# Moving the second stage's constants, first convolutions and first time step into the attention stage, with shared pools and single probability buffers

## The chip, the cores and the metric

The kernel runs on one core of one Trainium2 chip. The core has a matmul engine (TensorE, PE in the profile, with its weight loads shown as PEld), three engines for element-wise work (VectorE = DVE, ScalarE = ACT, GpSimd = POOL), and SyncE (SP), which issues nearly all transfers. Each engine works through its own instructions in program order; semaphores make one wait for another. All arithmetic is in 32-bit floats. The metric is the device time of one execution in microseconds: 3513.71 us, the median of three runs (3506.32 to 3513.76).

## What is computed

The input x has 8 sequences of 512 positions and 512 channels. Each position is layer-normed to xn, and two branches read xn: a selective state-space layer s, and a feed-forward layer whose gate is modulated by causal attention (16 heads of 32). Cut to what matters:

```python
xn = layernorm(x)
# attention, only as a rank-16 modulation of the gate
q, k, v = heads(rms(xn, ln1) @ Wq.T), heads(... Wk.T), heads(... Wv.T)
probs = softmax(causal(q @ k.T / sqrt(32)))
mod = 0.1 * tanh((probs @ v) @ Wo.T @ A)
h = rms(xn, ln2)
gate = silu(h @ W_in_base.T + mod * (h @ A) @ B)
g = silu(xn + (gate * (h @ W_up_base.T)) @ W_down.T)
# state space: 1024 channels, 16 states each
u, z = split(xn @ W_in.T)
xc = silu(causal_conv4(u) + conv_b)
B, C, dt = split(xc @ W_x.T);  dt = softplus(dt + mean(dt_bias))
h_t = exp(-exp(A_log) * dt_t) * h_{t-1} + dt_t * B_t * xc_t     # over 512 positions
s = ((sum_n C_t h_t + D * xc) * silu(z)) @ out_W.T
out = x + s * g
```

## The kernel before: how it is tiled and staged

There are two stages in one program, and both write their instructions in an order laid out by hand (a manual schedule): each engine runs what the Python code emits, in that order.

**Stage one** (the block with the pools a_w, a_row, a_big, a_small, a_p, a_ps_s, a_ps_mm, lines 80 to 489) does the norms and the attention for all eight sequences. Its unit is a group: one sequence b and one set hg of four heads, 32 groups in all. In group g the loop over s = 0..3 emits, for the group's own heads, `scores` for the s-th block of 128 queries (matmuls L292, mask L298, maximum L302, exponentials L308), and beside them, for the group before, ten `turn_probs` (four transposes each, L325, copied out at L331 on ACT or L329 on DVE), and, for the group before that, `divide` (L351 to L358). The list `slots` puts further products in between: queries and keys of the next group (L274), values (L258), transposes of the next sequence (L239). At the end of the group comes `attend` (L338) for the group before. `beside` places the norms of the next sequence and its loads. Exponentials are emitted two and three pieces after their scores. `modulation` (L366 to L376) closes each sequence and stores its 16 rows to the scratch scr_m; the transposed norms go to the scratch scr_x.

Products go to a ring of two PSUM banks (`bank`, pool a_ps_mm); scores go to three tiles of two banks each (a_ps_s). The probabilities of the s-th query block lie in a tile with tag p0 to p3 that has two buffers; the transposed ones in pt0 to pt3 with one each.

**Between the stages**, once stage one's pools are closed (from line 492 on): SP loads the constants of stage two (`const_tile`, L507), a_log is transposed (L536), stored (L540) and read back spread out by 16 loads (an, L543), the matrix sel is made by POOL and summed by DVE (L573 to L578), and the mean of dt_bias is formed (L564 to L568). Then the queue of parts for sequence 0 runs with nothing beside it: eight `conv_in` (product L590, bias L646, three taps L629, tanh L633, product with the sum L637, store to scr_c L641), and `step_size`: four projections (L792), softplus (L805 to L822), and a turn that stores to scr_p (L831) and loads bb, cc and dt (L833 to L837). The load of sequence 0's h and modulation (`load_h`, L518 and L521) is issued after the convolutions. Then come the first four scan inputs (L869).

**Stage two** (the loop at the end of the kernel) walks 64 scan steps per sequence: a scan on DVE (L898) over two channels' groups of states, decays on ACT (L878), products with B on DVE (L890) or POOL (L892) in turn, with C on POOL (L905), and sums over states on PE (L917). Between them it works off a queue of parts: gate products (`z_gate`, first one first, L590 and L658), `gate_up` (L678 to L704), the previous sequence's `finish` (L729, L745), and the next sequence's convolutions and step size. Its PSUM pool ps_mm is a ring of four banks; y, decay and a copy of B hold the other four.

Of the kernel before, what the change touches and what calls it, by code (L numbers as in the profile page):

```python
# [17 lines left out]
P = 128  # L18
NB = 8
# [20 lines left out]
def mamba_gated_ffn_kernel(  # L40
# [39 lines left out]
    with ExitStack() as c1:  # L80
        wp = c1.enter_context(tc.tile_pool(name="a_w", bufs=1))
        row = c1.enter_context(tc.tile_pool(name="a_row", bufs=8))
        big = c1.enter_context(tc.tile_pool(name="a_big", bufs=2))
        sm = c1.enter_context(tc.tile_pool(name="a_small", bufs=6))
        pp = c1.enter_context(tc.tile_pool(name="a_p", bufs=2))
        ps_s = c1.enter_context(tc.tile_pool(name="a_ps_s", bufs=3, space=PSUM))
        ps_mm = c1.enter_context(tc.tile_pool(name="a_ps_mm", bufs=2, space=PSUM))

        c1.enter_context(tc.manual_schedule())

        ZW = NH * R + R
        xts = {}

        def load_x(b):
            xts[b] = []
            for tt in range(TT):
                xt = row.tile([P, DM], F32, tag="xt", name=f"xt_{b}_{tt}")
                nc.sync.dma_start(xt, x[b, ts(tt, P), :])
                xts[b].append(xt)

        load_x(0)
        ln1 = wp.tile([P, KT], F32, tag="ln1", name="ln1")
        nc.sync.dma_start(ln1, ln1_w)
        ln2 = wp.tile([P, KT], F32, tag="ln2", name="ln2")
        nc.sync.dma_start(ln2, ln2_w)
        a_sb = wp.tile([P, KT, R], F32, tag="a_sb", name="a_sb")
        nc.sync.dma_start(a_sb, lora_a)
        wo = pp.tile([P, KT, DM], F32, tag="p3", name="wo")
        nc.sync.dma_start(wo, w_o)
        wv = pp.tile([P, KT, DM], F32, tag="p3", name="wv")  # L110
        nc.sync.dma_start(wv, w_v)
        wq = wp.tile([P, HG, KT, P], F32, tag="wq", name="wq")
        nc.sync.dma_start(wq, w_q)
        wk = wp.tile([P, HG, KT, P], F32, tag="wk", name="wk")
        nc.sync.dma_start(wk, w_k)

        eps_ln = wp.tile([P, 1], F32, tag="eps_ln", name="eps_ln")
        nc.vector.memset(eps_ln, LN_EPS)
        eps_rms = wp.tile([P, 1], F32, tag="eps_rms", name="eps_rms")
        nc.vector.memset(eps_rms, RMS_EPS)  # L120

        mask = wp.tile([P, P], F32, tag="mask", name="mask")
        nc.gpsimd.memset(mask, 0.0)
        nc.gpsimd.affine_select(
            out=mask, in_=mask, pattern=[[-1, P]], compare_op=ALU.is_ge,
            fill=MASKED, base=0, channel_multiplier=1,
        )


        zs = []  # L130
        for i in range(2):
            z = wp.tile([P, TT, HG, 4, 2 * R], F32, tag=f"z{i}", name=f"z{i}")
            nc.gpsimd.memset(z, 1.0)
            zs.append(z)
        woab = wp.tile([P, HG, 4, R], F32, tag="woab", name="woab")
        nc.gpsimd.memset(woab, 0.0)
        wz = wp.tile([P, KT, ZW], F32, tag="wz", name="wz")

        scale = 1.0 / math.sqrt(HD)

        xnT, xhT, norm, qks, probs, pts, outs, has, mos = {}, {}, {}, {}, {}, {}, {}, {}, {}

        def bank(name):
            return ps_mm.tile([P, 512], F32, tag="mm", name=name)

        def fold_weights():

            for hg in range(HG):
                ps = bank(f"ps_woa_{hg}")
                for jt in range(KT):  # L150
                    nc.tensor.matmul(
                        ps[:, :R], lhsT=wo[:, jt, ts(hg, P)], rhs=a_sb[:, jt, :],
                        start=(jt == 0), stop=(jt == KT - 1),
                    )
                for h in range(4):
                    nc.vector.tensor_copy(woab[ts(h, HD), hg, h, :], ps[ts(h, HD), :R])
            wvt = big.tile([P, HG, DM], F32, tag="hT", name="wvt", bufs=1)
            for hg in range(HG):
                ps = bank(f"ps_wvt_{hg}")
                for kt in range(KT):  # L160
                    nc.tensor.transpose(ps[:, ts(kt, P)], wv[:, kt, ts(hg, P)], ident)
                nc.scalar.copy(wvt[:, hg, :], ps)
            for kt in range(KT):
                ps = bank(f"ps_wz_{kt}")
                for hg in range(HG):
                    nc.tensor.matmul(
                        ps[:, ts(hg, 4 * R)], lhsT=wvt[:, hg, ts(kt, P)],
                        rhs=woab[:, hg].rearrange("p h r -> p (h r)"), start=True, stop=True,
                    )
                nc.vector.tensor_scalar(  # L170
                    wz[:, kt, : NH * R], ps[:, : NH * R], ln1[:, kt : kt + 1], None, ALU.mult
                )
                nc.vector.tensor_scalar(
                    wz[:, kt, NH * R :], a_sb[:, kt, :], ln2[:, kt : kt + 1], None, ALU.mult
                )
            for w, f in ((wq, scale), (wk, 1.0)):
                for kt in range(KT):
                    nc.vector.tensor_scalar(
                        w[:, :, kt, :], w[:, :, kt, :], ln1[:, kt : kt + 1], f,
                        ALU.mult, ALU.mult,  # L180
                    )

        def statistics(b):

            st = {}

            def moments(tt):
                if tt == 0:
                    st["mv"] = sm.tile([P, TT, 2], F32, tag="mv", name=f"mv_{b}")
                bn = sm.tile([P, nc.vector.BN_STATS_DIM], F32, tag="bn", name=f"bn_{b}_{tt}")  # L190
                nc.vector.bn_stats(out=bn, in_=xts[b][tt])
                nc.vector.bn_aggr(out=st["mv"][:, tt, :], in_=bn)

            def deviation():
                st["sd"] = sm.tile([P, TT], F32, tag="sd", name=f"sd_{b}")
                nc.scalar.activation(st["sd"], st["mv"][:, :, 1], AF.Sqrt, bias=eps_ln)

            def variance():
                mv = st["mv"]
                rstd = stats[:, b, :, 1]  # L200
                nc.vector.reciprocal(rstd, st["sd"])
                v2 = sm.tile([P, TT], F32, tag="v2", name=f"v2_{b}")
                nc.vector.tensor_tensor(v2, mv[:, :, 1], rstd, ALU.mult)
                nc.vector.tensor_tensor(v2, v2, rstd, ALU.mult)
                st["v2"] = v2

            def root():
                st["sd2"] = sm.tile([P, TT], F32, tag="sd2", name=f"sd2_{b}")
                nc.scalar.activation(st["sd2"], st["v2"], AF.Sqrt, bias=eps_rms)

            def ends():
                nc.vector.tensor_copy(stats[:, b, :, 0], st["mv"][:, :, 0])
                rs2 = sm.tile([P, TT], F32, tag="rs2", name=f"rs2_{b}")
                nc.vector.reciprocal(rs2, st["sd2"])
                norm[b] = [rs2]

            return [lambda tt=tt: moments(tt) for tt in range(TT)], [
                deviation, variance, root, ends,
            ]

        def normalise(b, tt):

            if tt == 0:
                xnT[b] = big.tile([P, KT, S], F32, tag="xnT", name=f"xnT_{b}", bufs=1)
                xhT[b] = big.tile([P, KT, S], F32, tag="xhT", name=f"xhT_{b}")
            n = row.tile([P, DM], F32, tag="xn", name=f"xn_{b}_{tt}", bufs=5)
            nc.vector.tensor_scalar(  # L227
                n, xts[b][tt], stats[:, b, tt, 0:1], stats[:, b, tt, 1:2],
                ALU.subtract, ALU.mult,
            )  # L230
            h = row.tile([P, DM], F32, tag="xh", name=f"xh_{b}_{tt}", bufs=5)
            nc.gpsimd.tensor_scalar(h, n, norm[b][0][:, tt : tt + 1], None, ALU.mult)  # L232
            norm[b].append((n, h))

        def turn(b, kt, i):

            ps = bank(f"ps_x{i}_{b}_{kt}")
            for tt in range(TT):
                nc.tensor.transpose(ps[:, ts(tt, P)], norm[b][1 + tt][i][:, ts(kt, P)], ident)  # L239
            if i == 0:  # L240
                nc.vector.tensor_copy(xnT[b][:, kt, :], ps)
                if kt == KT - 1:
                    nc.sync.dma_start(scr_x[b][:, :KT, :], xnT.pop(b))
                return
# [882 lines left out]
```

## Time and profile before

| | |
|---|---|
| profiled execution | 3509.93 us |
| its span, first to last instruction | 3508.2 us |
| mean granted TensorE clock | 0.961 |
| PE, weight loads | 3258.3 us (93%), 1472.0 us (42%) |
| DVE, ACT, POOL | 2533.5 us (72%), 1398.2 us (40%), 1908.4 us (54%) |
| one sequence in stage one (95 to 196 us) | 101 us, PE busy 89.5, DVE 62.8, ACT 55.8 |
| stage two's middle (1500 to 2000 us) | PE busy 488.1 of 500, DVE 387.9, POOL 354.9 |
| HBM traffic | 507 MB, 145 GB/s over the span |

How to read it: busy time is the sum of an engine's instruction times; the shares are averages over stages with different limits, so a stage is read from its own window. A line number such as L590 is a line of the kernel before. A row "x4" stands for four instructions taken together; a product of 32-bit floats shows as two instructions for each matmul in the code. The chain of waits goes back from the last instruction to what released it, so it says at each time which work the end depended on. A window row gives the busy time of each engine in a stretch and the clock that TensorE was granted there.

### The profile page before, as it was taken

The page shows a single profiled execution, that of the slowest core. Times are in us where ns is not written, and L with a number is a line of the kernel's source. Part 1 is how long each engine was busy: PE and PEld are TensorE (multiplying, and loading weights), DVE is VectorE, ACT ScalarE, POOL GpSimd, SP SyncE. Part 2 cuts the span into 40 slices and gives each one's busy share as a digit, 9 for nine tenths or more (in the row PEclk, how much of TensorE's full clock was granted, in tenths as well). Part 3 has the DMA queues.
Part 4 walks back from the last instruction along what each step waited for, and adds up shares of the span by engine and source line. Part 5 has one row for each costly group of instructions (what it writes and reads, how often), then busy time and mean ns, then how long its engine had stood idle before and what let it go on. Part 6 is the DMA issues. An engine that isn't in the chain of part 4 may idle for free.

```text
span 3508.2 us, 34088 instructions
## 1 busy us (share of the span) xinstructions
PE 3258.3 (93%) x12186; PEld 1472.0 (42%) x12186; DVE 2533.5 (72%) x2767; ACT 1398.2 (40%) x2343; POOL 1908.4 (54%) x859
## 2 busy tenths in 40 slices
PE   7988889896688899999999999999999999999999
PEld 4544545453333344344343434434343434344334
DVE  5666666654488878877887787788778868878871
ACT  3555555553233433433343333334333433333330
POOL 2111111100277777667667766777676767678870
PEclk8999999998799899999999999999999999999999
DMA  2000000001575696678569866867687597679652
GB/s 109 25 37 37 37 15 36 25 25 31 153 184 161 161 216 188 191 167 218 167 164 218 214 176 158 208 195 192 161 204 189 156 212 212 166 176 227 180 141 78
DMA packets 274842, 509.52 MB, mean 145 GB/s; under 512 B 24152, under 2 KB 155736, under 8 KB 270064
## 3 DMA queue, kind: packets, MB, share of 16 engines
q1 hardware_dynamic: 273520, 498.96, 54.5%
q0 software_dynamic: 1152, 8.39, 0.6%
q8 instruction: 96, 1.57, 0.2%
q14 instruction: 74, 0.61, 0.1%
HBM read 464.46 MB, written 42.81 MB: 145 GB/s over the span
## 4 chain that ended last, share of the span: by engine, by line
PE 58%; DVE 17%; POOL 8%; ACT 7%; issue 5%; DMA 4%; SPq 1%; POOLq 0%; ACTq 0%; DVEq 0%
PE ps_acc L729 11%; PE ps_gu L678 9%; DVE x L898 9%; POOL x L905 6%; PE ps_in L590 6%; PE ps_out L745 6%; PE y L917 5%; ACT decay L878 3%; PE ps_q L274 3%; PE ps_pt L325 3%; PE ps_k L274 3%; DVE conv L629 3%; PE s L292 3%; DMA win<-in_w_in 3%; PE ps_p L792 2%
## 5 line engine op out<-in xcount | busy, mean ns | idle before, releaser
L905 POOL TENSOR_TENSOR x<-x,cc 128x1024 f32<-128x1024 f32 x512 | 1206.9, 2357 | 689.4 <-DVE x L898 673.7
L898 DVE TENSOR_TENSOR_SCAN x<-decay,x 128x1024 f32<-128x1024 f32 x512 | 1169.9, 2285 | 189.7 <-ACT decay L878 188.5
L878 ACT ACTIVATE decay<-dt,an 128x511 f32<-128x511 f32 x1024 | 707.5, 691 | 1204.3 <-DVE x L898 1160.8
L678 PE MATMUL ps_gu<-ht,wgu 128*128 128x512 f32 x2048 | 938.6, 608 | 0.0
L892 POOL TENSOR_TENSOR x<-x,bb 128x1024 f32<-128x1024 f32 x256 | 603.4, 2357 | 79.3 <-DMA x<-scr_c 79.3
L678 PEld LDWEIGHTS ps_gu<-ht,wgu 128*128 128x128 f32 x2048 | 386.9, 194 | 536.0 <-issue 506.9
L590 PE MATMUL ps_in<-xnt,win 128*128 128x512 f32 x1024 | 467.9, 605 | 45.5 <-DMA win<-in_w_in 45.5
L729 PE MATMUL ps_acc<-m,wd 128*128 128x512 f32 x1024 | 451.8, 595 | 0.0
L917 PE MATMUL y<-x,sel 128*32 128x512 f32 x2048 | 308.8, 623 | 66.9 <-POOL x L905 66.9
L890 DVE TENSOR_TENSOR x<-x,dtb_ps 128x1024 f32<-128x1024 f32 x256 | 309.1, 1207 | 41.1 <-DMA x<-scr_c 38.5
L590 PEld LDWEIGHTS ps_in<-xnt,win 128*128 128x128 f32 x1024 | 195.9, 194 | 301.9 <-issue 272.7
L729 PEld LDWEIGHTS ps_acc<-m,wd 128*128 128x128 f32 x1024 | 191.0, 190 | 243.4 <-issue 242.2
L232 POOL TENSOR_SCALAR xh<-xn,rs 128x512 f32<-128x512 f32 x32 | 51.3, 1605 | 443.2 <-DVE xn L227 443.2
L308 ACT ACTIVATE p<-s,mx 128x384 f32<-128x384 f32 (+3 forms) x512 | 242.5, 529 | 76.4 <-DVE mx L302 74.2
L325 PE MATMUL ps_pt<-ident,p 128*128 128x128 f32 x1280 | 203.9, 283 | 25.5 <-ACT pt L331 8.8
L745 PE MATMUL ps_out<-xc,wout 128*128 128x512 f32 x512 | 226.9, 594 | 0.0
L302 DVE TENSOR_REDUCE mx<-s 128x2 f32<-128x256 f32 (+3 forms) x256 | 211.0, 824 | 8.8
L629 DVE SCALAR_TENSOR_TENSOR conv<-ps_in,cw,conv 128x511 f32<-128x511 f32 (+2 forms) x192 | 143.5, 747 | 73.7 <-ACT conv L646 69.1
L325 PEld LDWEIGHTS ps_pt<-ident,p 128*128 128x128 f32 x1280 | 140.8, 141 | 132.3 <-issue 45.9
L298 DVE TENSOR_TENSOR s<-s,mask 128x256 f32<-128x256 f32 x256 | 109.3, 427 | 108.8 <-PE s L292 107.2
L917 PEld LDWEIGHTS y<-x,sel 128*32 128x32 f32 x2048 | 61.4, 110 | 285.2 <-issue 148.7
L331 ACT COPY pt<-ps_pt 128x512 f32<-128x512 f32 x224 | 129.7, 587 | 111.4 <-PE ps_pt L325 110.9
(130 smaller groups left out, 2382.2 us busy)
## 6 DMA issues: line engine op xcount, KB each, us to landing
x<-scr_c SPq DMA_DIRECT2D x512, 512.0 KB
wgu<-in_w_ffn SPq DMA_DIRECT2D x128, 512.0 KB
win<-in_w_in SPq DMA_DIRECT2D x128, 256.0 KB
wd<-in_w_ffn SPq DMA_DIRECT2D x128, 256.0 KB
scr_c<-xc SPq DMA_DIRECT2D x64, 256.0 KB
wout<-in_out_w SPq DMA_DIRECT2D x32, 512.0 KB
xt<-in_x SPq DMA_DIRECT2D x32, 256.0 KB
scr_x<-xnT SPq DMA_DIRECT2D x8, 1024.0 KB
```

The costliest lines, as they stand in the source:

```text
L325: nc.tensor.transpose(ps[:, ts(j, P)], probs[b, hg, qt][:, h, ts(kt, P)], ident)
L590: nc.tensor.matmul(ps, lhsT=w[:, kt, :], rhs=xnt[b][:, kt, :], start=(kt == 0), stop=(kt == KT - 1))
L629: nc.vector.scalar_tensor_tensor(acc[:, sh:], ps[:, : S - sh], cw[:, d, k : k + 1], acc[:, sh:], ALU.mult, ALU.add,)
L678: nc.tensor.matmul(ps, lhsT=w[:, which, kt, :], rhs=ht[b][:, kt, :], start=(kt == 0), stop=(which == 1 and kt == KT - 1),)
L729: nc.tensor.matmul(st["acc"], lhsT=w[:, j, :], rhs=mlp[b, f], start=(f == 0), stop=(f == NF - 1))
L745: nc.tensor.matmul(st["ps"], lhsT=w[:, d, :], rhs=xc[b, d], start=(d == 0), stop=(d == ND - 1))
L878: nc.scalar.activation(decay[:, n, 1:], spread[b][2][:, 1:], AF.Exp, scale=an[:, g // 4, g % 4 : g % 4 + 1])
L890: nc.vector.tensor_tensor(t, t, dtb_ps.unsqueeze(1).to_broadcast([P, 2, S]), ALU.mult)
L892: nc.gpsimd.tensor_tensor(t, t, spread[b][0].unsqueeze(1).to_broadcast([P, 2, S]), ALU.mult)
L898: nc.vector.tensor_tensor_scan(t, decay.rearrange("p i t -> p (i t)"), t, 0.0, ALU.mult, ALU.add)
L905: nc.gpsimd.tensor_tensor(t, t, spread[b][1].unsqueeze(1).to_broadcast([P, 2, S]), ALU.mult)
L917: nc.tensor.matmul(y[ts(j, QD), :], lhsT=sel[:, i0 + n, :], rhs=xs[k - 3 + j][:, n, :], start=(i0 + n == 0), stop=(i0 + n == 3),)
```

## The change

It moves what lay between the stages into stage one, and moves the pools so that this is possible.

- The pools of stage two that the moved work needs (w, act, xcp, a new tmc, and two of its four PSUM banks as ps_1) are opened before stage one and live through both stages. Stage one draws its rows (xt, xn, xh) from xcp's ring of 16 (a tile of 512 floats), its transposed norms from act, and its products from ps_1. The weights win move from wst to w.
- To make room, p0 to p3 and mo have one buffer instead of two; wo and wv lie in the buffers of p3 and pt0.
- `turn_probs` no longer takes four (head, query block) pairs in a row for a key block, but the four heads of one (key block, query block) pair; the ten are ordered by query block, so that p0 is read up first and p3 last. The copy writes 4 pieces of 128 into the transposed tile. (kt + qt) % 3 == 2 goes to DVE.
- `constants` is split in three and emitted in sequence 0: loads in group (0, 0) at s = 3, decay rates in (0, 1) at s = 2, selection in (0, 2) at s = 2.
- Sequence 0's xn and the first three weights are loaded in group (7, 1). A pair of convolutions stands after s = 1 and s = 3 in groups (7, 2) and (7, 3), in one two-bank tile of the scores' ring.
- The four projections stand in the trailing group (which only turns and attends for (7, 3)), one after each s, and the turn of the step size after its attend.
- Stage two's remaining pools are opened after stage one. Its four banks are now ps_1 and ps_2 with two each, taken in turn. `load_h(0)` is issued after the whole step size, just ahead of the first scan inputs.

```diff
+    def bank(name):
+        if banks["special"]:
+            return banks["special"](name)
+        banks["n"] += 1
+        pool = banks["second"] if banks["second"] and banks["n"] % 2 else ps_1
+        return pool.tile([P, 512], F32, tag="mm", name=name)
...
-            pr = pp.tile([P, 4, w], F32, tag=f"p{qt}", name=f"p_{b}_{hg}_{qt}")
+            pr = pp.tile([P, 4, w], F32, tag=f"p{qt}", name=f"p_{b}_{hg}_{qt}", bufs=1)
...
-        turns = [(kt, i) for kt in range(TT) for i in range(TT - kt)]
+        turns = [(kt, qt) for qt in range(TT) for kt in range(qt + 1)]
...
+        const_steps = dict(zip(((0, 0, 3), (0, 1, 2), (0, 2, 2)), constants()))
+        sizes = step_size(0)
+
+        def convolutions(i):
+
+            pair = ps_s.tile([P, 2, 512], F32, tag="s", name=f"s_conv_{i}")
+            for d in (2 * i, 2 * i + 1):
+                banks["special"] = lambda name, d=d: pair[:, d % 2, :]
+                for delay, f in piece(conv_in(0, d)[0][2]):
+                    after(delay, f)
+                banks["special"] = None
+                if d + 3 < ND:
+                    load_win(0, d + 3)
+
+        def steps_of_time(i):
+            if i == 0:
+                pair = ps_s.tile([P, 2, 512], F32, tag="s", name="s_steps")
+                steps["pair"] = pair
+            n = 1 if i == TT else 0
+            banks["special"] = lambda name: steps["pair"][:, n, :]
+            part = sizes[0][i] if i < TT else sizes[1][0]
+            for delay, f in piece(part[2]):
+                after(delay, f)
+            banks["special"] = None
...
+            if at == 2 and (b, hg, s) in const_steps:
+                const_steps[b, hg, s]()
             if n == NB:
+                if (hg, s, at) == (1, 0, 0):
+                    load_xn(0)
+                    for d in range(3):
+                        load_win(0, d)
+                if hg >= 2 and s % 2 == 1 and at == 3:
+                    convolutions((hg - 2) * 2 + s // 2)
                 return
...
+                if g == len(items):
+                    steps_of_time(s)
...
+            if g == len(items):
+                steps_of_time(TT)
...
-    for d in range(ND):
-        queue.extend(conv_in(0, d))
-    sizes = step_size(0)
-    while state["run"] < len(queue):
-        run_part()
-        next_chunk()
     load_h(0)
-    flush()
-    queue.extend(sizes[0])
-    while state["run"] < len(queue):
-        run_part()
-    flush()
-    queue.extend(sizes[1])
-    run_part()
```

## The prediction

> **What bounds the kernel now.** I read three things in this order: the slices of the page, the windows around the dip that they show, and the chain of waits through that dip. The slices are 87.7 us each (span 3508.2 us over 40).
>
> ```profile
> PE   7988889896688899999999999999999999999999
> PEclk8999999998799899999999999999999999999999
> ```
>
> TensorE is nearly full from the twelfth slice on; that is stage two. It is at 6 to 9 tenths, mostly 8, in stage one, and at 6 in the tenth and eleventh slice, 789 to 965 us, where stage one ends and stage two begins. Windows there (busy us and instruction counts of PE, weight load, DVE, ACT, POOL, then granted clock, DMA share, GB/s):
>
> ```profile
> 771.00:796.00 25.00, 22.30 (x136) 12.63 (x138) 15.37 (x30) 13.03 (x28) 0.00 (x0) 1.00 0.01 3
> 796.00:830.50 34.50, 32.41 (x245) 17.68 (x238) 25.47 (x49) 22.51 (x47) 0.00 (x0) 1.00 0.10 31
> 830.50:841.80 11.30, 8.91 (x76) 5.49 (x76) 2.90 (x8) 5.71 (x11) 0.00 (x0) 1.00 0.01 2
> 841.80:868.00 26.20, 4.08 (x18) 2.22 (x18) 7.76 (x19) 1.08 (x3) 4.84 (x8) 0.57 0.24 42
> ```
>
> Up to 830.5 us PE is the bound (89 to 94% busy), with DVE at 74% and ACT at 65% in the last two groups of heads. After 841.8 nobody is busy: a serial chain runs. The chain of waits names its links (start, duration, what):
>
> ```profile
> 839.30 2.40 PE o_ps L338 x32
> ...
> 849.39 1.77 DMA al<-in_a_log
> ...
> 864.72 2.94 DMA win<-in_w_in
> 867.66 0.48 issue
> 868.14 5.91 PE ps_in L590 x8
> ...
> 904.91 10.89 PE ps_p L792 x50
> 915.82 0.23 DVE sp L805
> ...
> 921.47 1.61 DMA scr_p<-pt
> ...
> 924.99 0.52 SPq L869
> ...
> 928.16 10.80 DMA win<-in_w_in
> 939.00 6.34 PE ps_in L590 x8
> ...
> 947.73 2.29 DVE x L898
> ```
>
> The last attend ends at 841.7 (839.30 + 2.40). The chain then goes through the last modulation (to 849.4), the constants (15.3, 849.39 to 864.72), the first weights and first product (9.4), eight convolutions (30.8, to 904.9), the rest of the time-step projection (10.9), softplus (3.9), turn, store and loads (13.4, to the first scan, at 933.14 in the timeline), and a first gate that holds the second scan until 947.73. That is **106.0 us** from the last attend to the second scan, after which the scans run regularly. The change attacks this stretch; what it costs is paid in stage one.
>
> **1. What remains between last attend and second scan.** Let T be the end of the last attend in the changed kernel. There the projections stand before the attend and softplus follows them, so its 3.9 us are covered by the attend (2.4) but for 1.5. Turn 1.06, copy 0.6, issue 0.1: the store leaves at T+3.2, dt is issued by T+6.8 (SP took 0.6 for each of three, after 1.6 for the store). PE does the last divide only after that turn, at T+2.6, and from the same point in the trace (842.37) to the store of scr_m (847.71) took 5.3: T+8. Behind it on SP now stand the load of ht (1 MB) and two small modh loads, which before were issued at 894, under the convolutions; SP needed 1.5 for them, so the first scan input is issued at T+9.9. Before, issue to scan took 8.15 (924.99 to 933.14) behind 0.75 MB of bb, cc, dt; now 1 MB of ht is ahead. From 923.09 to 939.0 about 3.15 MB landed, 198 GB/s, so 0.25 MB more and a shorter head start cost 1.7. First scan T+19.7. The wait for the gate's weights behind the inputs is untouched, 14.6 (933.14 to 947.73): second scan at **T+34.3**. Saved here: 106.0 - 34.3 = **71.7**. Ends 65 (DMA slower) and 76 (ht overlaps).
>
> **2. Convolutions beside the last two groups.** Eight products of 8 matmuls; the same form of row (ps_k below, clock 1.00) is 3.45 to 3.70 for 8. 8 x 3.45 = 27.6 of PE. The other engines' share, from the groups of the stretch 841 to 950 us and PE's timeline:
>
> ```profile
> L629 DVE SCALAR_TENSOR_TENSOR conv<-ps_in,cw,conv 128x511 f32<-128x511 f32 (+2 forms) x24 | 18.0, 749 | 5.9 <-ACT conv L646 5.3
> L646 ACT ACTIVATE conv<-ps_in,cb,cw 128x512 f32<-128x512 f32 x8 | 6.1, 762 | 9.5 <-PE ps_in L590 9.5
> L637 DVE SCALAR_TENSOR_TENSOR xc<-ps_in,conv 128x512 f32<-128x512 f32 x8 | 5.5, 691 | 5.8 <-ACT ps_in L633 5.8
> L633 ACT ACTIVATE ps_in<-conv 128x512 f32<-128x512 f32 x8 | 4.8, 601 | 19.6 <-DVE conv L629 19.6
> 807.72 3.70 PE L274 MATMUL ps_k<-xhT,wk 128*128 128x512 f32 x8
> 897.91 1.42 PE L792 MATMUL ps_p<-wx,xc 128*128 128x33 f32 x12
> ```
>
> A pair of convolutions takes, from the end of its first product: bias 0.8, taps 2.35, tanh 0.65, silu 0.7, taps 2.35, tanh 0.65, silu 0.7 = 8.2, while PE is through its second product after 3.45. PE then does two turns and the scores (2.1), and its third turn waits for a probability bank whose copy stands on ACT behind the second tanh. I walked this group by group: about 2.7 us of PE waiting for a pair placed after s = 1, 1.5 after s = 3, less what those groups already waited: 5.5 in all. Cost **33.1**. Ends 26 (all waits fall into the 2 to 3 us a group that PE idles now) and 52 (DVE, which holds 13 us of own work in the last group of 14.7, becomes the bound and delays the maxima too).
>
> **3. Projections in the trailing group.** 64 matmuls. The row of 12 gives 0.118 each at full clock, the chain's 50 give 0.217 in the cold stretch. The Trainium skill (TensorE: Matmul & The Clock Gate, Part 1) says the clock is halved after an idle window and released by sustained work; the trailing group keeps PE at 79% with a granted 1.00, so I take 0.118: **7.6**; by the cold row it would be 13.9.
>
> **4. Constants in batch 0.** PE: eight transposes and one sum, 2.4 in the trace. DVE: four reductions of 1.0 that each wait for POOL's memset and select (1.24), so DVE is held some 6 us at once with the masks of scores queued behind it and PE behind those; PE rides over about half. SP's 16 an loads (6.4) stand only before loads for the next batch, not needed for 25 us. I take **5**, ends 2 and 9.
>
> **5. Single probability buffers and the new order of turns.** The question is whether an exponential now waits for the transposes of the previous group. Waits of ACT and PE, 100 to 830 us (total, times, longest):
>
> ```profile
> ACT p L308 <- DVE mx L302: 69.6, 96, 2.2
> ACT p L308 <- PE ps_pt L325: 0.8, 1, 0.8
> PE ps_pt L325 <- ACT pt L331: 7.3, 17, 0.8
> ```
>
> Each exponential waits for the mask and maximum, 1.7 us (0.44 + 1.24) after its scores. In the new order the transposes that free p0, p1, p2 are a step earlier, and the last one for p3 directly follows the scores and takes 0.66. So nothing is late. A rule of the Trainium skill speaks against it: Perfetto Trace Analysis, Optimization Strategy, says equal gaps recurring on the engine to be saturated can mean too little room for the next tile. By it I would add 0.66 for each of 31 groups, 20 us; by the rows, nothing. I follow the rows. Copies stay 7 on ACT, 3 on DVE a group; strided ones cost nothing extra: the strided z copy takes 372 ns for 256 elements, the plain q copy 585 for 512. Shifted places: **+1**, ends -8 and +12.
>
> **6. Stage two** keeps each engine's order. Its four banks become two alternating pools; a few products per batch take a bank freed one to seven DVE instructions later. At the worst recurring one the bank is freed by a DVE instruction that ended at 1520.2 us, and PE needs it at 1522.1: nothing.
>
> **Sum:** -71.7 + 33.1 + 7.6 + 5 + 1 = -25.0, from the profiled execution's 3509.9 (span 3508.2) to 3484.9. The median of the runs shown is 3513.71, 3.8 above that execution; I forecast its counterpart, **3488**.
>
> **Rivals.**
> - **All of it fits.** The waits of step 2 fall into idle time, constants cost 2 and ht is hidden: 27 + 7 + 2 - 73 = -37, **3477**. For it: PE idles 2 to 3 us in each group. Against it: silu waits for tanh on both in-order engines.
> - **The convolutions choke the last groups.** DVE becomes the bound there, 52 in place of 33: **3507**, no change. For it: the 13 of 14.7 us. Against it: the group becomes 28 us long with DVE's 28.
> - **Slower: the order of turns stalls every group.** Turns (0,3) and (1,3), then the product for k, now take banks whose ACT copies stand behind exponentials, where one came from DVE before. Its place is each group's third step; at 1.5 us in 31 groups it costs 46: **3534**. It decides from 25/31 = 0.8 us a group. Against it: my count has the copy done 0.4 us before PE needs the bank. If the banks of step 6 bite, it ends there too.
> - **The work doesn't move at all:** excluded, since the instruction order already shows it in stage one.
>
> **Chances.** Forecast 0.60 (own range 3478 to 3499), all fits 0.17, choke 0.10, slower 0.10, rest 0.03. A measurement here can tell about 0.2%, 7 us. Faster by more: nearly all of the first two and two fifths of choke, 0.80; same 0.06; slower 0.14. Range 3471 to 3506.
>
> **What would show it.** From last attend to second scan about 34 us, with ht landing before the first x; the last attend ending near 888; two groups of about 36 and 32 us around 800 to 860; ps_p rows at 0.12; groups of 23 to 25 us elsewhere; no ACT p wait on PE. Wrong if a batch of stage one grows past its 101 us by 3 or more, if the last attend is later than 905, or if stage two is longer than before from its second scan.

## The result and the profile after

The changed kernel takes **3530.28 us** (median of 7 runs, 3516.24 to 3542.37) where the kernel before, beside it, takes 3513.01; the ratio is 1.0055, with a 95% interval of 1.0033 to 1.0077. It is slower by 17 us between the medians, 19 by the ratio. The forecast was 3488, and its range ended at 3506. Run once more among the experiments, it came to 1.0054 (1.0032 to 1.0075).

The profiled execution took 3532.69 us with a span of 3530.3, against 3508.2 before. Line numbers are now those of the changed kernel. Its slices, 88.3 us each:

```profile
PE   7888899897688899999999999999999999999999
PEclk9999999998699899999999999999999999999999
```

PE's dip in the eleventh slice is still there, and the clock in that slice is lower, 6 tenths instead of 7. Below are the stretches around it in the view of windows (busy us and counts of PE, weight load, DVE, ACT, POOL; then granted clock, DMA share, GB/s). They run from attend to attend: group (7,1), groups (7,2) and (7,3), the trailing group, and what follows up to the second scan. (The last attend ends at 939.5 us, 1.3 us into the last row.)

```profile
783.80:809.30 25.50, 23.06 (x149) 13.04 (x151) 16.25 (x31) 14.21 (x32) 0.00 (x0) 1.00 0.00 1
809.30:860.60 51.30, 39.88 (x156) 18.32 (x156) 21.15 (x37) 17.63 (x34) 0.00 (x0) 0.83 0.09 27
860.60:908.90 48.30, 35.12 (x143) 17.02 (x142) 23.86 (x40) 16.98 (x32) 0.00 (x0) 0.79 0.10 33
908.90:938.20 29.30, 27.09 (x157) 23.04 (x160) 7.17 (x17) 7.79 (x14) 0.00 (x0) 0.60 0.05 19
938.20:969.90 31.70, 11.15 (x51) 5.16 (x44) 9.75 (x23) 6.54 (x10) 4.63 (x2) 0.67 0.84 240
```

Groups (7,2) and (7,3) take 51 and 48 us, not 36 and 32, and PE idles in about a quarter of them. DVE is busy for less than half of each, so it isn't full. The clock falls to 0.8, and to 0.60 in the trailing group, where PE is busy nearly all the time but slowly. Stretch by stretch, the marks are the starts of three attends, the end of the last attend, and the start of the second scan. The attends are these, first in the kernel before, then in the changed one (the last attend of the kernel before, at 839.30, stands in the prediction's chain):

```profile
794.07 2.36 PE L338 MATMUL o_ps<-pt,z 128*32 128x512 f32 x32
828.13 2.36 PE L338 MATMUL o_ps<-pt,z 128*32 128x512 f32 x32
```

```profile
809.26 2.36 PE L857 MATMUL o_ps<-pt,z 128*32 128x512 f32 x32 [0.29 <-DVE mod_t L894]
908.89 2.36 PE L857 MATMUL o_ps<-pt,z 128*32 128x512 f32 x32
935.76 3.73 PE L857 MATMUL o_ps<-pt,z 128*32 128x512 f32 x32
```

The last column is the change in a second profiled execution of the same changed kernel (the one run among the experiments), with a span of 3517.8 us.

| stretch | before, us | after, us | change | forecast | change, second execution |
|---|---|---|---|---|---|
| up to the attend that opens group (7,2) | 794.1 | 809.3 | +15.2 | +6 | +2.2 |
| groups (7,2) and (7,3) | 34.1 | 99.7 | **+65.6** | +33.1 | **+63.6** |
| trailing group with the last attend | 13.6 | 30.6 | +17.0 | +7.6 | +7.7 |
| last attend to second scan | 106.0 | 30.4 | -75.6 | -71.7 | -73.6 |
| second scan to the end | 2560.5 | 2560.5 | 0 | 0 | +9.7 |

The changes add up to +22.2 and +9.6; the spans differ from the one before by 22.1 and 9.6. The saving came as forecast. What was paid for it ahead of the gap was twice as much in the first execution. Only the excess in the two groups with convolutions is there in both. The first, third and last row differ by 9 to 13 us between two executions of the same program. PE's timeline through the first pair (start, duration, operation, idle time before it and what ended it):

```profile
819.61 3.60 PE L186 MATMUL s_conv<-xnt,win 128*128 128x512 f32 x8
827.12 6.49 PE L186 MATMUL s_conv<-xnt,win 128*128 128x512 f32 x8 [3.91 <-ACT s_conv L229]
...
838.69 0.66 PE L843 MATMUL ps_pt<-ident,p 128*128 128x128 f32 x4 [3.35 <-ACT pt L850]
```

The second product of the pair waits 3.91 us, and not for weights: what releases it is ACT's L229, the tanh of the *first* convolution. Then it runs at little more than half speed, 6.49 where the first took 3.60. The timelines of ACT and DVE in the same stretch:

```profile
823.24 0.78 ACT L242 ACTIVATE conv<-s_conv,cb,cw 128x512 f32<-128x512 f32 x1 [1.76 <-PE s_conv L186]
826.46 0.60 ACT L229 ACTIVATE s_conv<-conv 128x512 f32<-128x512 f32 x1 [1.71 <-DVE conv L225]
833.71 0.78 ACT L242 ACTIVATE conv<-s_conv,cb,cw 128x512 f32<-128x512 f32 x1 [6.64 <-PE s_conv L186]
837.52 0.60 ACT L229 ACTIVATE s_conv<-conv 128x512 f32<-128x512 f32 x1 [3.04 <-DVE conv L225]
```

```profile
824.05 2.31 DVE L225 SCALAR_TENSOR_TENSOR conv<-s_conv,cw,conv 128x511 f32<-128x511 f32 x3 [2.38 <-ACT conv L242]
834.51 0.69 DVE L233 SCALAR_TENSOR_TENSOR xc<-s_conv,conv 128x512 f32<-128x512 f32 x1 [8.14 <-ACT conv L242]
835.12 2.31 DVE L225 SCALAR_TENSOR_TENSOR conv<-s_conv,cw,conv 128x511 f32<-128x511 f32 x3
```

Bias, taps and tanh of the first convolution (823.24 to 827.06) fill exactly the time in which PE stands. The silu of the first (L233) doesn't start after its tanh at 827.06 but at 834.51, when the second product and its bias are done. So the two convolutions of a pair run one after the other, 19.2 us from 819.61 to 838.8, where the forecast had them overlap. The view of waits, 800 to 940 us (total, times, longest), shows that it is the same four times:

```profile
PE s_conv L186 <- ACT s_conv L229: 15.7, 4, 3.9
PE ps_pt L843 <- ACT pt L850: 6.7, 2, 3.4
PE ps_pt L843 <- ACT o L862: 4.0, 2, 2.2
```

After the last attend the chain of waits reads as forecast: the store of the modulation, SP's issues, the gate's weights, and the second scan.

```profile
945.15 3.04 DMA scr_m<-mod_t
...
950.75 10.81 DMA win<-in_w_in
...
961.70 5.76 PE ps_in L186 x8
...
969.85 2.29 DVE x L494
```

### The profile page after: what moved, and what is told of

Same layout as the page of the kernel before. It is cut to its first block, busy times and chain, and to the rows that moved or that the text cites. A ratio compares the mean times of both kernels' runs of the same rounds, so it can differ in the third digit from the quotient of the medians.

```text
span 3530.3 us, 34084 instructions
## 1 busy us (share of the span) xinstructions
PE 3278.7 (93%) x12186; PEld 1483.2 (42%) x12186; DVE 2528.4 (72%) x2766; ACT 1395.4 (40%) x2343; POOL 1909.0 (54%) x860
## 4 chain that ended last, share of the span: by engine, by line
PE 36%; DVE 17%; POOL 6%; ACT 5%; DMA 4%; issue 3%; SPq 0%; POOLq 0%; DVEq 0%; ACTq 0%
PE ps_acc L325 11%; DVE x L494 11%; PE ps_gu L274 8%; PE ps_out L341 6%; PE ps_in L186 6%; POOL x L501 5%; ACT decay L474 4%; PE y L513 4%; DVE conv L225 3%; DMA win<-in_w_in 3%; DMA x<-scr_c 1%; POOL x L488 1%; PE ps_p L388 1%; DVE x L486 1%; PE ps_gu L283 1%
## 5 line engine op out<-in xcount | busy, mean ns | idle before, releaser
L186 PE MATMUL ps_in<-xnt,win 128*128 128x512 f32 x960 | 442.9, 609 | 44.7 <-DMA win<-in_w_in 44.6
L513 PE MATMUL y<-x,sel 128*32 128x512 f32 x2048 | 301.2, 612 | 63.3 <-POOL x L501 63.3
L186 PEld LDWEIGHTS ps_in<-xnt,win 128*128 128x128 f32 x960 | 184.5, 195 | 288.0 <-issue 281.7
L225 DVE SCALAR_TENSOR_TENSOR conv<-ps_in,cw,conv 128x511 f32<-128x511 f32 x168 | 125.5, 747 | 66.6 <-ACT conv L242 62.6
```

Of the source, the lines that this page charges most:

```text
L186: nc.tensor.matmul(ps, lhsT=w[:, kt, :], rhs=xnt[b][:, kt, :], start=(kt == 0), stop=(kt == KT - 1))
L513: nc.tensor.matmul(y[ts(j, QD), :], lhsT=sel[:, i0 + n, :], rhs=xs[k - 3 + j][:, n, :], start=(i0 + n == 0), stop=(i0 + n == 3),)
```

## Experiments

Both products of a pair write into one tile, `pair`, one bank each. The schedule emits one piece at a time (a turn, a product, the scores of a block), and just ahead of each piece what earlier pieces have left for it with `after`. The first convolution leaves its taps and tanh for the next piece, and that is the second product. The theory to be tested, **T**: a wait is set by tile and by order of emission. The first convolution's taps, which read the pair's tile, and its tanh, which writes to it, are emitted ahead of the second product, so the second product waits for them although it writes to the other bank; and the idle PE is then clocked down. The main rival, **D**, is the "choke" of the prediction: the chain on DVE and ACT would hold PE whatever the tiles. **W**: the second product waits for its weights. All ratios are to the kernel before, run on the same chip.

### A tile for each convolution

```diff
-            pair = ps_s.tile([P, 2, 512], F32, tag="s", name=f"s_conv_{i}")
             for d in (2 * i, 2 * i + 1):
-                banks["special"] = lambda name, d=d: pair[:, d % 2, :]
+                own = ps_s.tile([P, 2, 512], F32, tag="s", name=f"s_conv_{d}")
+                banks["special"] = lambda name, own=own: own[:, 0, :]
```

> Each convolution gets a tile of the scores' ring of its own; a pair shares none; all else as in the changed kernel. Theory T (the shared tile makes the pair's second product wait 3.9 us for the first one's tanh, and the idle PE is then clocked down): the four waits of 3.9 us go, the second products take 3.6 instead of 6.5, groups (7,2) and (7,3) take about 38 and 34 us instead of 51.3 and 48.3, the trailing group runs at a clock near 1.00 with projections at 0.12 each instead of 0.216 and takes about 19 instead of 26.9; time about 3490 (0.993 to 0.995 of the kernel before). Rival D (the chain of bias, taps, tanh and silu on ACT and DVE is what holds PE, whatever the tiles): waits move to the turns and the next scores, the two groups stay above 45 us each, time 3520 or more. Rival W (the second product waits for its weights): no change, 3530.

Measured: ratio **0.9958** (0.9940 to 0.9976), 12 runs, median 3487.37. Against the changed kernel's 1.0055 that is about 34 us less, from two lines. PE's timeline of this version through the first pair, and the windows of its two groups and its trailing group:

```profile
822.06 7.03 PE L186 MATMUL s_conv<-xnt,win 128*128 128x512 f32 x16
833.83 0.66 PE L843 MATMUL ps_pt<-ident,p 128*128 128x128 f32 x4 [2.61 <-ACT pt L850]
```

```profile
811.70:848.60 36.90, 34.03 (x156) 16.64 (x156) 21.25 (x37) 17.08 (x34) 0.00 (x0) 0.95 0.12 38
848.60:882.60 34.00, 29.27 (x144) 15.20 (x143) 23.79 (x40) 16.75 (x33) 0.00 (x0) 0.90 0.14 47
882.60:899.90 17.30, 14.90 (x145) 12.74 (x148) 6.62 (x13) 6.18 (x11) 0.00 (x0) 1.00 0.09 32
```

The two products are one run of 7.03 us, no wait names L229, and the groups take 36.9 and 34.0. DVE did as much work in the two groups as in the changed kernel (21.25 and 23.79 us against 21.15 and 23.86), and so did ACT (17.08 and 16.75 against 17.63 and 16.98), so the work of these engines was not what held PE for the other 29 us. By the PE column, 17.0 of these were idle time and 11.7 were busy time, that is, the lower clock. T holds, D as the main cause and W fall.

### Both products ahead of the element work, in the shared tile

```diff
             for d in (2 * i, 2 * i + 1):
-                banks["special"] = lambda name, d=d: pair[:, d % 2, :]
-                for delay, f in piece(conv_in(0, d)[0][2]):
-                    after(delay, f)
-                banks["special"] = None
+                piece(product, d)
                 if d + 3 < ND:
                     load_win(0, d + 3)
+            for d in (2 * i, 2 * i + 1):
+                for delay, f in conv_in(0, d, pair[:, d % 2, :])[0][2]():
+                    after(delay + d % 2, f)
```

(`product` is the eight matmuls of L186; `conv_in` takes the finished bank.)

> The pair keeps its shared tile; both products are emitted before the first bias, and the element work of the two follows. Theory T in its narrow form (a wait is set by tile and by the order of emission, so that a product emitted after the first one's tanh waits for it): the wait of 3.9 us is gone though the tile is shared; time 3485 to 3495, within 5 us of the version with a tile each. If the two banks of one tile can't be worked on by PE and ACT at once for a reason of the hardware, the second product would still stretch and the time would stay above 3515. Rival D: above 3515. Rival W: 3530.

Measured: ratio 1.0033 (1.0019 to 1.0047). PE's timeline, and the two biases in ACT's:

```profile
820.27 7.03 PE L958 MATMUL s_conv<-xnt,win 128*128 128x512 f32 x16
832.39 0.66 PE L843 MATMUL ps_pt<-ident,p 128*128 128x128 f32 x4 [3.37 <-ACT pt L850]
835.98 5.81 PE L794 MATMUL ps_k<-xhT,wk 128*128 128x512 f32 x8 [2.92 <-ACT pt L850]
```

```profile
827.34 1.45 ACT L242 ACTIVATE conv<-s_conv,cb,cw 128x512 f32<-128x512 f32 x2 [4.14 <-PE s_conv L958]
```

Half of the expectation came true: with no tanh emitted between the products, the wait is gone though the tile is shared, so it is the order of emission that set the wait. (Whether ACT and PE can work in the two banks at the same time isn't seen here, since no bias is emitted before both products.) The time did not follow. The element work now starts only after both products: the first bias 7.1 us and the first taps 8.6 us after the first product's start (827.34 and 828.82), against 3.6 and 4.5 with a tile each (825.70 and 826.51). The first bias reads only the first bank, yet it starts when the second product is done (820.27 + 7.03): a shared tile ties the pair together in either order. PE then stands behind ACT's copies, 14.6 us in five places against 5.2 in two. By the traces the two groups and the trailing group take 120.2 us against 90.5 with a tile each; about half of that difference (33.6 against 19.6 us) is the trailing group, at a granted clock of 0.59.

### One convolution after each step

```diff
-                if hg >= 2 and s % 2 == 1 and at == 3:
-                    convolutions((hg - 2) * 2 + s // 2)
+                if hg >= 2 and at == 3:
+                    convolutions((hg - 2) * 4 + s)
```

(`convolutions` now emits one, in a tile of its own.)

> One convolution after each of the eight steps of groups (7,2) and (7,3), each with a tile of its own, instead of pairs after every second step. Theory T: no wait of 3.9 us, PE idle under 1.5 us at a time, clock near 1.00, the two groups about 34 and 32 us, time 3484 to 3492. Rival D: DVE has 24 us of taps and silu in these two groups whatever the spacing, so above 3510.

Measured: ratio 0.9996 (0.9980 to 1.0011), groups of 45.8 and 40.9 us. That is worse than pairs with a tile each, and T's 34 and 32 did not come. PE's waits in the two groups and the trailing one:

```profile
PE ps_pt L843 <- DVE pt L848: 6.2, 3, 2.9
PE ps_pt L843 <- ACT pt L850: 3.8, 2, 1.9
PE s_conv L186 <- DVE xc L233: 3.7, 2, 2.5
```

Here rival D has its share: a copy on DVE stands behind 2.3 us of taps, and PE behind the copy. In a pair the second product covers the first one's taps; alone, each convolution shows its own. (That this is the whole difference is argued, not shown.)

### The order of turns, without and with single buffers

The kernel before, with nothing but `turn_probs` and the list `turns` of the changed kernel; and then with `bufs=1` for p0 to p3 too (wo and wv placed as in the changed kernel). Theory **O**: the order lengthens a batch; rival **B**: the single buffers do.

> The kernel before with nothing but the new order and shape of turn_probs (p0 to p3 keep two buffers; all constants, convolutions and steps stay between the stages). Theory O (the order of turns is what lengthens a batch of stage one by 1.1 us, through the bank of ps_k and a slower clock): a batch takes about 101.9 to 102.3 instead of 101.1 on average, 7 to 9 us over stage one, time 3515 to 3522, ratio 1.002 to 1.0025. Rival B (the single buffers do it): no change, ratio 1.000. The prediction's row had +1.

> The kernel before with the new order of turns and single buffers for p0 to p3. Theory O: as with the order alone, within 2 us of it by the batches of the trace. Rival B: an exponential or its mask waits for the transposes of the group before; a batch 1 us or more longer than with the order alone, ratio 1.002 or more only here.

Measured: order alone 1.0017 (1.0009 to 1.0026), some 6 us; with single buffers 1.0002 (0.9992 to 1.0012), nothing. B falls: in the changed kernel too, 100 to 800 us, the one wait of exponentials that the view of waits lists is

```profile
ACT p L828 <- DVE mx L822: 36.9, 108, 1.0
```

and none is for the transposes that free a buffer. O can't be settled. One group in each batch (the third of the four, counted from the first attend) takes about 24.0 us in both versions and in the changed kernel where it took 23.5 before. The rest of a batch moves with the clock: the five batches in the middle take 511.3 us in one execution of the changed kernel and 505.5 in the other, 504.7 before. Why the version with single buffers shows nothing of the half microsecond per batch is not known.

### The second tanh later

```diff
-            nc.scalar.activation(ps, acc, AF.Tanh)
+            if not late:
+                tanh()
...
+            if late:
+                return [(1, taps), (2, tanh), (3, silu), (5, store)]
             return [(1, taps), (2, silu), (4, store)]
```

On top of a tile each, for the second of a pair. Theory **A**: what is left is ACT waiting at a tanh in program order, with a copy behind it.

> A tile each, and the second convolution of a pair emits its tanh one piece after its taps and its silu one piece after that, so that ACT copies a turned block before it comes to the tanh that waits for the taps. Theory A (what is left of stalls in the version with a tile each, 2.6 us of PE for ACT's copy in four places, is ACT standing at a tanh in program order): these waits fall under 1 us, the two groups take about 34 and 32, time 3476 to 3484. Rival D (the DVE chain holds PE anyway): waits move to the scores, time as with a tile each, 3487.

Measured: ratio 0.9965 (0.9952 to 0.9978), as with a tile each. The two groups take 34.7 and 35.1, together 69.8 against 70.9. The waits of 2.6 us (two of them by the view of waits of a tile each, 5.2 us in 2, not four) did not fall under 1 us as A expected. They moved on by one instruction and are 2.03 us now, still behind ACT's copy:

```profile
827.29 3.70 PE L800 MATMUL ps_k<-xhT,wk 128*128 128x512 f32 x8 [2.03 <-ACT pt L856]
860.67 0.66 PE L849 MATMUL ps_pt<-ident,p 128*128 128x128 f32 x4 [2.03 <-ACT pt L856]
```

ACT's timeline ahead of the first of them has the second tanh, waiting for the taps, and the copy right behind it:

```profile
826.13 0.60 ACT L233 ACTIVATE s_conv<-conv 128x512 f32<-128x512 f32 x1 [1.97 <-DVE conv L225]
826.66 1.06 ACT L856 COPY pt<-ps_pt 128x512 f32<-128x512 f32 x2
```

So one copy passes, and the next one stands behind the tanh. The mechanism is A's, the outcome in time is D's, and D's place (the scores) is not where the waits went.

### Loads ahead of the gap, and the convolutions over four groups

Three versions on top of the last one. First `load_h(0)` in group (7,1) and the first gate's weights behind the last convolution (theory **G**: the second scan waits only for weights behind other loads). Then either one pair in each of the four groups, or the first gate and up weights ahead of three of the scan inputs, with the product for the mean of dt_bias one group later.

```diff
-    load_h(0)
     for k in range(4):
         load_scan(k)
...
+                if (hg, s, at) == (1, 2, 0):
+                    load_h(0)
...
-                if d + 3 < ND:
+                if d + 3 <= ND:
                     load_win(0, d + 3)
```

> As the version before it, and besides the load of h for sequence 0 is issued in group (7,1) and the first gate's weights right after the last convolution, both ahead of the time step's loads. Theory G (between first and second scan the first gate waits only for its weights, which stand behind 1 MB of h and 2 MB of scan inputs): first scan about 4 us and second scan about 14 to 16 us earlier, counted from the last attend; time 3462 to 3470. Rival: the next products wait for their weights (wgu) instead, and stage two is longer from its second scan by most of it; 3475 to 3482.

> As the version with early loads, but one pair of convolutions after the last step of each of the four groups of the last sequence, instead of two pairs in each of the last two; xn and the first weights are loaded from (7,0) on. Theory A (a pair costs 7.1 us of PE and little else where ACT and DVE have room): the four groups take about 8 us each over 28.1, 19.5, 23.5 and 14.7 less the stalls, last attend 3 to 6 us earlier than with two pairs a group, time 3476 to 3482 where the version with early loads has 3483. Rival D (the groups are held by DVE: 22 us busy of 34): last attend 8 us earlier or more.

> As the version with early loads, with two further edits. The first two weights of the gate and up products are issued after the first scan input and ahead of the other three; expected: ps_gu starts about 8 us earlier than in the version with early loads (there 25.4 us after the last attend, a wait of 13.4), time 5 to 8 lower, 3475 to 3478, unless the scans, whose inputs come 5 us later, set the pace at the start of stage two (then no change). And the sum over dt_bias is formed one group later than its DVE part, so that PE does not wait for it: the wait of 2.5 us in group (0,1) goes and the product for k after it takes 3.7 instead of 5.4; first and second attend about 4 us earlier.

Measured: early loads 0.9933 (0.9916 to 0.9950), a pair per group 0.9913 (0.9889 to 0.9938), weights first 0.9911 (0.9890 to 0.9931). With early loads the first scan is 16.3 us and the second 20.4 after the last attend, where the version without them has 20.1 and 34.4. But PE then waits for the next weights, so its products start only 6.5 us sooner (25.3 after the attend instead of 31.8). PE's timeline with early loads, and with the weights first:

```profile
902.24 5.43 PE L186 MATMUL ps_in<-xnt,win 128*128 128x512 f32 x8
921.07 9.75 PE L280 MATMUL ps_gu<-ht,wgu 128*128 128x512 f32 x16 [13.40 <-DMA wgu<-in_w_ffn]
```

```profile
892.30 5.43 PE L186 MATMUL ps_in<-xnt,win 128*128 128x512 f32 x8
902.15 8.80 PE L280 MATMUL ps_gu<-ht,wgu 128*128 128x512 f32 x16 [4.42 <-DMA wgu<-in_w_ffn]
```

There the wait is 4.42 in place of 13.40, and the products start 16.3 us after the attend. So G was right about the scans, and the rival about the wait of the next products, which took the place of the first until it was moved too. Which of the two sets the time is open: early loads gain 11 us by the ratio over the version before them, give or take some 8 by the two intervals, and that has room for the 14.0 of the second scan and for the 6.5 of the products. The last two versions can't be told from early loads by their times, for the intervals overlap.

A pair in each group makes the last sequence's groups 30.5, 33.0, 27.7 and 22.5 us long, 30.5 more than before in all, close to PE's own 28.1 (4 x 7.03). (Before they take 23.5, 25.6, 19.4 and 14.7; the expectation has them in another order, with 28.1 for 25.6.) Two pairs in each of two groups cost 39.0 (23.6, 25.5, 36.4, 36.6). The traces so put 8.5 us on the crowding of pairs, which was D's mark. Of these 5.6 are busy time of PE (111.0 us against 105.4): in the four groups the granted clock is 1.00, where the two crowded ones had 0.95 and 0.86. The rest is idle time.

### All of it

> All that helped, together: a tile each, the second tanh later, one pair in each group of the last sequence, h and the first gate's weights early, the first gate and up weights ahead of the later scan inputs, the sum over dt_bias one group later. If the gains add: 8 us below the version with wgu first by the last groups, time 3470 to 3474, ratio 0.988 to 0.990. If stage two's start is set by the scans, the two gains overlap: 3476 to 3480.

> As the version with all of it, but the second tanh again straight behind its taps. Theory A' (with one pair in a group, at its last step, the attend and its copy follow, so a tanh that holds ACT for 2.5 us delays a turned block only once in a group): four waits of 1.4 to 2.6 us return, 3 to 8 us slower by the last groups. Rival: they fall into the attend's 2.4 us; within 2 us by the trace.

Both came to 0.9914 (0.9894 to 0.9933, and 0.9891 to 0.9938), medians 3479.55 and 3478.76, some 30 us faster than the kernel before. The gains of the last two versions don't show as a sum: in its trace the version with all of it starts ps_gu at 897.89, 4.3 us before the one with weights first alone, less than these runs can tell. The four groups take 113.7 us with the later tanh and 114.6 with the early one, so the rival holds and the later tanh makes no difference to be seen.

## Why the prediction was wrong

**Step 1, the gap: right.** Forecast 34.3 us to the second scan; measured 30.4, 32.4 in the second execution, and 35.6 in the version with a tile each. Its links were the ones named.

**Step 2, the convolutions: the step that failed.** "A pair of convolutions takes ... while PE is through its second product after 3.45", and with that 33.1 us. This took the second product as free to run while ACT and DVE work on the first. In the program it stands behind the first one's tanh, for `pair` is one tile and `piece` emits what is due before the new product. Both could be read from the code. The measured term is 65.6, and 63.6 in the second execution; with a tile each it is 36.8, inside the step's range and 3.7 from its value. So the walk through the groups was sound and its premise was not. The rows of the kernel before couldn't warn of it, since each of its eight convolutions had a one-bank tile of its own.

**Step 3, the projections: the wrong one of two prices in the first execution, the right one in the second.** The Trainium skill (TensorE: Matmul & The Clock Gate, Part 1) has the clock fall after an idle window and rise with sustained work; I argued that the trailing group keeps PE busy and took 7.6. The fall came: PE had waited 3.9 us ahead of the last convolution and 2.2 at the start of the trailing group. The rise did not come in this trace, which so differs from the page. PE has no wait from 914.05 to 935 us, and the granted clock stays near one half:

```profile
914.00:935.00 21.00, 20.95 (x101) 20.32 (x102) 3.19 (x9) 3.99 (x7) 0.00 (x0) 0.52 0.04 13
```

The row of projections in the changed kernel (count, busy us, mean ns; they overlap, so that the busy time is less than count times mean) is

```profile
L388 PE MATMUL s_steps<-wx,xc 128*128 128x33 f32 x64 | 13.8, 393 | 0.0
```

while with a tile each, where only a wait of 1.9 us stands just before, it is

```profile
L388 PE MATMUL s_steps<-wx,xc 128*128 128x33 f32 x64 | 7.5, 272 | 0.0
```

So the two prices of the prediction, 7.6 and 13.9, both occur. The program alone does not decide which: in the second execution of the changed kernel PE has the same waits (four of 3.9 us, then 2.2), but the clock is back at full some 10 us after the trailing group's start, the projections take 7.9, and the row costs 7.7 more than before. Its windows, the two groups and the trailing one:

```profile
796.31:893.93 97.62, 73.20 (x296) 34.82 (x296) 45.02 (x77) 34.57 (x66) 0.00 (x0) 0.83 0.09 30
893.93:915.15 21.22, 18.66 (x173) 15.15 (x172) 7.09 (x16) 7.70 (x14) 0.00 (x0) 0.92 0.07 26
```

Why the clock rose in one execution and not in the other is not known.

**Step 4, the constants: inside its range, near the upper end.** 5 was forecast, with 2 to 9. PE's timeline in group (0,1) has a wait for the sum over dt_bias, and after it the product for k at the low clock:

```profile
87.13 0.35 PE L162 MATMUL ps_dtb<-dts,ones 128*128 128x1 f32 x2 [2.48 <-DVE dts L160]
87.35 5.38 PE L794 MATMUL ps_k<-xhT,wk 128*128 128x512 f32 x8
```

With 1.2 us of transposes that is 5.5 over a product at full clock, and the next group is 2.4 longer: about 8. In the version where the sum came a group later, that wait is gone (one of 1.56 us for a copy of a_log's transposes is left) and k took 3.70. The first attend as a whole is no measure, for it came at 96.6 and at 88.4 in two executions of the same kernel.

**Step 5, turns and buffers: right in sign of the buffers, open in size.** No exponential waits for transposes, and single buffers added to the new order cost nothing; the Trainium skill's rule of equal gaps (Perfetto Trace Analysis, Optimization Strategy), by which it would have been 20 us, was rightly set aside. The order was put at +1 with -8 to +12; it cost 0 to 6 by the two runs, and the changed kernel was 7 us longer over six batches in one profile and 4 in the other.

**Step 6, stage two: right as far as can be told.** From the second scan on it takes 2560.5 us before and in the first execution of the changed kernel, but 2570.2 in the second. Versions that leave this stage alone lie between 2556.2 (the new order alone) and 2570.4 (the later tanh), so a cost of some us would not be seen. Of the prediction's signs of being wrong, the last attend came later than 905 in both executions (939.5 and 915.2), and stage two was longer in the second.

**The rivals.** The slower one, put at 3534 by turns that stall every group, gives nearly the measured time for a reason that did not occur: no batch grew by 3 us. The choke was the nearest in place, but it named DVE's load, and the tile was what cost most; of its mechanism at most some 8 us remained. A rival was missing: that two products in one tile are not independent.

## What to carry to other kernels

When work is placed beside other work, first read each moved instruction's waits in the program order of the new place, and ask of every tile it touches who wrote or read it last by emission: two banks in one tile are one thing to wait for. An overlap that holds in the old place, with a buffer for each, is no evidence for the new place. And a wait on TensorE can cost more than its length, for the clock fell after every one of 3.9 us here; behind such a wait carry both prices, at full and at half clock, because two executions of one program took one each.

## What the runs showed of the hardware that was not expected

Every stall of 3.9 us of PE was followed by a product of 8 matmuls at 5.2 to 6.7 us, where 3.6 is the full-clock row: all eight in two executions of the changed kernel. Shorter stalls did it too, but not always: after 2.6 us the product for k took 5.38 with a tile each, and after 2.03 us it took 3.70 in the version with the later tanh and 5.40 in the one with early loads, in the same place. Nor did steady work always bring the clock back: it stayed near one half through 21 us in which PE was busy. Executions of the same program also differ in where the clock is low: the groups with transposes of the next sequence take mostly 28.4 to 28.8 us or 30.9 to 31.0. The two profiled executions of the changed kernel have spans 12.5 us apart: the second comes to its second scan 22.3 us earlier and is 9.7 longer after it. So one profile tells less of a change of 5 us than the sum of its local waits does.
